# A macaron layer on one core: the shared expert's 64 rest rows in two halves of the array, with the attention order moved along

## The chip, the cores and the metric

The kernel runs on one core of a Trainium2 chip. The metric is the device time of one execution in microseconds (us), lower is better. A core has TensorE (PE, its weight loads are shown as PEld), VectorE (DVE), ScalarE (ACT), GpSimd (POOL) and SyncE (SP, which issues most DMAs). Products land in PSUM, which has eight banks here: two tiles of two banks under the tag `big`, two of one bank under `mm`, two of one bank under `aux`.

## The reference

All is float32. With 16 x 256 = 4096 tokens of 256 channels:

```python
x = x + 0.5 * ffn(layernorm(x))      # ffn adds its own input
x = x + attention(layernorm(x))
x = x + 0.5 * ffn(layernorm(x))

def ffn(inp):
    x = w_norm * inp * rsqrt(mean(inp * inp) + eps)
    # 32 experts, top 4 of each token, at most 128 tokens an expert, hidden width 176
    out = sum over chosen experts of weight * (silu(x @ w_gate[e]) * (x @ w_up[e])) @ w_down[e]
    sh = (silu(x @ sw_gate) * (x @ sw_up)) @ sw_down        # shared expert, hidden width FS = 704
    return inp + out + sigmoid(x @ w_shared_gate) * sh
```

Attention has 16 heads of width 32 (8 for keys and values), rotary positions, a tanh soft cap and a causal softmax. The change is in the shared expert, `sh`, and in the order of the attention stage.

## The kernel before

The 4096 tokens are handled as 8 groups (`NG`) of 4 tiles (`GT`) of 128 tokens. A feed-forward has a route stage (`route`, router logits and top 4), a slot stage (`slots`, which tokens each expert takes), an expert stage (`expert`, 32 times: gather by indirect DMA, gate and up products, down product, scatter-add by indirect DMA into `acc`), and the shared expert (`shared`). The attention stage has 32 units (batch element b and half of the heads m of a group), each with scores in two parts, values and, after every second unit, an output product (`project_out`).

TensorE's order is the program's order throughout; in attention that holds for DVE, ACT and POOL too, and in the expert stage for POOL.

**The shared expert.** `shared` is a generator for one group. Its hidden width 704 is five chunks of 128 and a rest of `FR` = 64. For each chunk it makes the gate and up products of 512 tokens into a `big` tile `pg` (L399), then ACT makes a tanh (L403) and DVE two operations (L404, L405), and the result stands in `act`. The rest chunk, the sixth, holds gate in 64 partitions and up in the other 64 of one half of `pg`. Then for each of the 4 tiles it adds six products (five chunks and the rest) in one PSUM tile `po` (L411, tag `mm`), and DVE adds the sum to x (L415). The rest's product runs over 128 rows, of which 64 rows of weights in `swd` are zero (L150). A float32 product is two passes, two instruction records, on TensorE.

**Filling.** `Fill` hands out the pieces of `shared` between other work. A `take(us)` adds to a budget and runs pieces until it is used up; each piece yields its assumed cost (3.4 us for a chunk, 1.7 for the rest chunk, 2.6 for a tile). The takes are listed in the constants: `ROUTE_FILL` per piece of routing, `SLOT_FILL` and `ROW_FILL` per piece of the slot stage, `FIRST_FILL`, then `EXPERT_FILL` for each of 34 steps of the expert loop. `SUM_FILL` stands behind the last expert of the first feed-forward: it covers the time in which the scatter-adds end, `read_sums` loads them, `add_sums` adds them on POOL (L474), and `moments` and `root` prepare the layer norm of attention.

**Attention's order.** `project(g)` is the chain of a group into attention: read the sums, add them, moments, the normalised rows `a` on ACT (L493), two transposes of half a group each (`pta` L503, copied by ACT to `hT` L504), then the projections `pq` (L512) and `pv` (L540). For unit k with g, j = divmod(k, 4), the loop runs pieces of group g + 1 (`mine`), group g + 2 (`ahead`) and of the routing of groups g - 1 and g - 2 (`routing`, with the transposes `pt` L267 and ACT's `xnT` L270 as one piece) at places written out by hand. `PROJECT_PIECES` says how many pieces of `mine` stand before the second part of the scores and how many behind the values.

## Time and profile before

| what | value |
|---|---|
| median of 3 runs | 1059.1 us (1058.38 to 1059.3) |
| the profiled execution | 1057.55 us |
| its span in the profile | 1055.8 us |
| granted TensorE clock | 1.0 |
| TensorE busy, idle | 1025.7 us, 30.1 us |
| `pg` products (L399) | 704 records, 318.6 us |
| `po` products (L411) | 768 records, 178.9 us |
| scatter-adds (L462) | 64, 1587 ns each on POOL |

By the trace, the route stage of the first feed-forward lies at 0 to 110 us, the slots up to 166, the experts up to 327, the way into attention up to 383, attention up to 735, and the second feed-forward behind it.

How to read it: a line of a timeline is start, duration, engine, line of the kernel, operation, tile written <- tiles read, shape, and how many instructions are merged; in brackets stands the idle time before it and what ended it. A shape like 32*128 of a matmul is rows*columns of the array in use. The duration of a matmul record runs beyond the start of the next, as the array is pipelined, so the cost of a stream is read from start to start.

### The profile page before, as it was taken

To read this page: it belongs to the slowest core of one execution; us is meant where nothing else is said; L and a number is where in the kernel's file an instruction comes from. 1 tells how busy PE (TensorE), PEld (TensorE's weight loads), DVE (VectorE), ACT (ScalarE), POOL (GpSimd) and SP (SyncE) were. 2 spreads that over 40 slices of the span, in tenths; PEclk is the share of its full clock that TensorE was granted. 3 is DMA by queue.
4 is the path that set the end of the run, shared out by engine and by line. 5 is a ranking of instruction groups with operands and counts; after the bars stand their busy time and mean duration, and the time that the engine had idled before them with its cause. 6 is when DMAs were issued, how large, how long until landed. Compare 5 with 4: busy or idle time off the path is not lost.

```text
span 1055.8 us, 15603 instructions
## 1 busy us (share of the span) xinstructions
PE 1025.7 (97%) x5432; PEld 647.2 (61%) x5432; DVE 630.9 (60%) x1684; ACT 399.1 (38%) x761; POOL 496.2 (47%) x548
## 2 busy tenths in 40 slices
PE   8999999999999999989999999999999999999998
PEld 5656656876866445545455555555566476867765
DVE  4964674544343546777878879774756635444453
ACT  3442111222221245675748476667310122232201
POOL 4410102455552478688676767564101234455450
PEclk9999999999999999999999999999999999999999
DMA  8731802878872100000101010000300157788572
GB/s 280 214 122 46 247 6 61 167 164 178 170 163 31 39 21 1 21 21 1 43 1 43 2 43 1 24 23 2 100 30 1 34 128 161 169 162 175 100 226 103
DMA packets 137869, 92.97 MB, mean 88 GB/s; under 512 B 80512, under 2 KB 135104, under 8 KB 137792
## 3 DMA queue, kind: packets, MB, share of 16 engines
q1 hardware_dynamic: 125504, 74.16, 25.6%
q0 software_dynamic: 12288, 17.83, 10.1%
q8 instruction: 43, 0.70, 0.3%
q14 instruction: 34, 0.28, 0.1%
HBM read 60.99 MB, written 30.97 MB: 87 GB/s over the span
## 4 chain that ended last, share of the span: by engine, by line
PE 87%; DVE 5%; ACT 3%; issue 1%; POOL 1%; DMA 1%; POOLq 0%; ACTq 0%
PE pg L399 26%; PE po L411 15%; PE pge L446 8%; PE pq L512 8%; PE poa L625 5%; PE sc L561 5%; PE poe L459 5%; PE y L607 3%; PE den L607 3%; PE pv L540 3%; PE pl L283 2%; PE pte L438 1%; PE pa L369 1%; ACT a L493 1%; PE pt L267 1%
## 5 line engine op out<-in xcount | busy, mean ns | idle before, releaser
L399 PE MATMUL pg<-xnT,sw 128*128 128x512 f32 x704 | 318.6, 597 | 2.0 <-DVE act L405 2.0
L399 PEld LDWEIGHTS pg<-xnT,sw 128*128 128x128 f32 x704 | 130.0, 190 | 138.3 <-issue 130.1
L462 POOL DMA_INDIRECT acc<-y,idx x64 | 101.4, 1584 | 179.6 <-DVE y L461 62.0
L411 PE MATMUL po<-swd,act 128*128 128x256 f32 x768 | 178.9, 383 | 3.9 <-DVE x L415 1.3
L403 ACT ACTIVATE act<-pg 128x512 f32<-128x512 f32 x96 | 57.2, 596 | 285.2 <-PE pg L399 285.2
L411 PEld LDWEIGHTS po<-swd,act 128*128 128x128 f32 x768 | 142.9, 190 | 34.1 <-issue 10.6
L404 DVE SCALAR_TENSOR_TENSOR act<-act,pg 128x512 f32<-128x512 f32 x96 | 65.7, 685 | 154.1 <-ACT act L403 154.1
L568 ACT ACTIVATE p<-sc 128x512 f32<-128x512 f32 (+1 forms) x128 | 97.0, 809 | 100.3 <-PE sc L561 99.8
L422 POOL DMA_INDIRECT xg<-xtab,idx x64 | 68.1, 1064 | 75.4 <-DVE idx L377 56.5
L446 PE MATMUL pge<-xgT,wgu 128*112 128x128 f32 (+1 forms) x768 | 95.9, 275 | 7.6 <-issue 5.6
L573 POOL TENSOR_SCALAR_AFFINE_SELECT p<-p 128x512 f32<-128x512 f32 x128 | 81.5, 663 | 44.2 <-ACT p L571 42.6
L571 ACT ACTIVATE p<-p 128x512 f32<-128x512 f32 (+1 forms) x128 | 101.0, 845 | 0.0
L446 PEld LDWEIGHTS pge<-xgT,wgu 128*112 128x112 f32 (+1 forms) x768 | 88.6, 182 | 11.2 <-issue 11.2
L415 DVE SCALAR_TENSOR_TENSOR x<-po,sg,x 128x256 f32<-128x256 f32 x64 | 30.9, 483 | 75.0 <-PE po L411 74.8
L441 ACT ACTIVATE xgT<-pte,wnorm 128x128 f32<-128x128 f32 x128 | 39.9, 365 | 74.8 <-PE pte L438 74.8
L405 DVE TENSOR_TENSOR act<-act,pg 128x512 f32<-128x512 f32 x96 | 65.7, 685 | 2.3
L520 POOL TENSOR_TENSOR qs<-qs,kc 128x512 f32<-128x512 f32 x48 | 61.5, 1282 | 10.3 <-DVE qs L515 10.3
L459 PE MATMUL poe<-wd,sie 112*128 112x256 f32 x256 | 65.9, 379 | 0.1
L561 PE MATMUL sc<-qT,kT 32*128 32x256 f32 (+1 forms) x512 | 64.2, 533 | 1.7 <-ACT p L568 1.3
L512 PE MATMUL pq<-hT,wq 128*128 128x512 f32 x128 | 60.9, 599 | 0.0
L625 PE MATMUL poa<-wo,yT 128*128 128x256 f32 x256 | 59.7, 386 | 1.2 <-DVE qT L519 1.2
L625 PEld LDWEIGHTS poa<-wo,yT 128*128 128x128 f32 x256 | 47.2, 190 | 18.8 <-issue 3.8
(109 smaller groups left out, 1342.6 us busy)
## 6 DMA issues: line engine op xcount, KB each, us to landing
xtab<-xr SPq DMA_DIRECT2D x16, 576.0 KB
acc<-zero SPq DMA_DIRECT2D x2, 4224.0 KB
a<-acc SPq DMA_DIRECT2D x16, 512.0 KB
wgu<-in_L_ffn_w_gate SPq DMA_DIRECT2D x64, 112.0 KB
wgu<-in_L_ffn_w_up SPq DMA_DIRECT2D x64, 112.0 KB
wd<-in_L_ffn_w_down SPq DMA_DIRECT2D x64, 112.0 KB
wgu<-in_L_ffn_w_gate SPq DMA_DIRECT2D x64, 64.0 KB
wgu<-in_L_ffn_w_up SPq DMA_DIRECT2D x64, 64.0 KB
```

The lines of the kernel that those rows point to most:

```text
L399: nc.tensor.matmul(pg[:, s, :], lhsT=sw[:, c, w0 : w0 + P], rhs=xnT[:, c, cols], start=(c == 0), stop=(c == 1))
L411: nc.tensor.matmul(po, lhsT=act[:, k, t * P : (t + 1) * P], rhs=swd[:, k, :], start=(k == 0), stop=(k == len(FC) - 1),)
L422: nc.gpsimd.indirect_dma_start(out=xg, out_offset=None, in_=xtab[n], in_offset=bass.IndirectOffsetOnAxis(ap=idx[:, e : e + 1], axis=0), bo ...
L446: nc.tensor.matmul(pg[:fw, n_, :], lhsT=wgu[:, c, w0 : w0 + fw], rhs=xgT[:, c, :], start=(c == 0), stop=(c == 1))
L459: nc.tensor.matmul(po, lhsT=si[:, k, :], rhs=wd[:, k, :], start=(k == 0), stop=(k == 1))
L462: nc.gpsimd.indirect_dma_start(out=acc[n], out_offset=bass.IndirectOffsetOnAxis(ap=idx[:, e : e + 1], axis=0), in_=y, in_offset=None, boun ...
L512: nc.tensor.matmul(pq, lhsT=weights[:, c, :], rhs=hT[:, c, :], start=(c == 0), stop=(c == 1))
L561: nc.tensor.matmul(sc[i // 2][:, i % 2, 0 : 2 * w].rearrange("p (s t) -> p s t", s=2), lhsT=kT[r, m, t0 + k0 : t0 + k0 + P], rhs=qT[r, m, ...
L568: nc.scalar.activation(parts[h], sc[h][:, :, 0 : 2 * w], AF.Tanh, scale=QK_SCALE / SOFTCAP)
L571: nc.scalar.activation(parts[h], parts[h], AF.Exp, scale=SOFTCAP)
L573: nc.gpsimd.affine_select(out=diag, in_=diag, compare_op=ALU.is_ge, fill=0.0, base=0, pattern=[[0, 4], [1, P]], channel_multiplier=-1,)
L625: nc.tensor.matmul(po, lhsT=yT[:, c // 2, c % 2, qh * P : (qh + 1) * P], rhs=wo[:, c // 2, c % 2, :], start=(c == 0), stop=(c == 3),)
```

## The change

- The rest chunk's results for tiles 0 and 1 of a group stay in partitions 0 to 63 of `act`; those for tiles 2 and 3 go to partitions 64 to 127. `swd` holds the rest's weights twice, once in each half. The rest's products of the four tiles then run one after another, 64 rows each, alternating between the halves of the array, and open the sums (`start=True`); the other five products follow.
- For that, the four tiles' sums `pos` are open at the same time: two banks of one `big` tile, and two `aux` tiles where `wide()` says so or else the two banks of a second `big` tile.
- In such a group the rest chunk is made first of the six, with its ACT and DVE work in two halves. Tiles are taken in the order 0, 2, 1, 3. Costs become 3.4 for the first tile (with all the rest products) and 2.1 for the others; `EXPERT_FILL` of the first feed-forward becomes 2.05.
- `paired` holds for groups begun in the first feed-forward and from the end of attention on; a generator is made when its group begins. Other groups keep the old way, with a memset of the empty half of `act` in place of that of `swd`.
- In attention: the pieces of `mine` are swapped in unit 1; the normalised rows of `ahead` move to the end of j = 2, the first half of its transposes to the place behind the values at j = 3, the second stays at the end; the piece of `routing` with the first transposes moves behind the fill at j = 3, but for the last units.

The diff:

```diff
--- before.py
+++ after.py
@@ -41,7 +41,7 @@
-ROUTE_FILL, SLOT_FILL, FIRST_FILL, EXPERT_FILL, SUM_FILL, PROJECT_FILL = 3.0, 1.7, 6.0, (2.15, 2.3), 17.0, 1.5
+ROUTE_FILL, SLOT_FILL, FIRST_FILL, EXPERT_FILL, SUM_FILL, PROJECT_FILL = 3.0, 1.7, 6.0, (2.05, 2.3), 17.0, 1.5
 LAST_FILL = 8.0
 MASK_FILL, ROW_FILL = 4.0, 3.2
 WARM = (9, 3)
@@ -147,8 +147,8 @@
     swd = cpool.tile([P, len(FC), C], F32, name="swd")
     nc.sync.dma_start(swd[:, 0:5, :], sw_down[0:640, :].rearrange("(c p) d -> p c d", p=P))
-    nc.gpsimd.memset(swd[FR:P, 5, :], 0.0)
-    nc.sync.dma_start(swd[0:FR, 5, :], sw_down[640:FS, :])
+    for h in range(2):
+        nc.sync.dma_start(swd[h * FR : (h + 1) * FR, 5, :], sw_down[640:FS, :])
     for g in range(2, NG):
         load_x(g)
     nc.sync.dma_start(kc[:, P:], consts[:, P:])
@@ -379,42 +379,67 @@
-    def shared(pool, g, last):
+    def shared(pool, g, last, paired, wide):
         sg = stat.tile([P, GT], F32, name="sg")
         nc.scalar.activation(sg, gate[:, g * GT : (g + 1) * GT], AF.Tanh, scale=0.5)
         nc.vector.tensor_scalar(sg, sg, 1.0, 0.125, ALU.add, ALU.mult)
         act = pool.tile([P, len(FC), GW], F32, name="act")
         cols = slice(g * GW, (g + 1) * GW)
-        for k, (f0, fw) in enumerate(FC):
+        rest = len(FC) - 1
+        for k in [rest, *range(rest)] if paired else range(rest + 1):
+            f0, fw = FC[k]
             pg = big.tile([P, 2, GW], F32, tag="big", name="pg")
-            if fw == P:
-                at = [f0, FC[-1][0] + f0]
-                b = pg[:, 1, :]
-            else:
-                at = [2 * f0]
-                b = pg[fw : 2 * fw, 0, :]
+            at = [f0, FC[-1][0] + f0] if fw == P else [2 * f0]
             for s, w0 in enumerate(at):
                 for c in range(2):
                     nc.tensor.matmul(
                         pg[:, s, :], lhsT=sw[:, c, w0 : w0 + P], rhs=xnT[:, c, cols], start=(c == 0), stop=(c == 1)
                     )
-            si = act[:fw, k, :]
-            nc.scalar.activation(act[:, k, :], pg[:, 0, :], AF.Tanh, scale=0.5)
-            nc.vector.scalar_tensor_tensor(si, si, 1.0, pg[:fw, 0, :], ALU.add, ALU.mult)
-            nc.vector.tensor_mul(si, si, b)
+            if fw == P:
+                parts = [(act[:, k, :], pg[:, 0, :], pg[:, 1, :])]
+            elif paired:
+                halves = [(slice(h * fw, (h + 1) * fw), slice(h * GW // 2, (h + 1) * GW // 2)) for h in range(2)]
+                parts = [(act[r, k, t], pg[0:fw, 0, t], pg[fw : 2 * fw, 0, t]) for r, t in halves]
+            else:
+                nc.gpsimd.memset(act[fw:P, k, :], 0.0)
+                parts = [(act[0:fw, k, :], pg[0:fw, 0, :], pg[fw : 2 * fw, 0, :])]
+            for si, a, b in parts:
+                nc.scalar.activation(si, a, AF.Tanh, scale=0.5)
+                nc.vector.scalar_tensor_tensor(si, si, 1.0, a, ALU.add, ALU.mult)
+                nc.vector.tensor_mul(si, si, b)
             yield 1.7 * len(at)
-        for t in range(GT):
+        if paired:
+            pos = big.tile([P, 2, GW], F32, tag="big", name="pos")
+            pos = [pos[:, h, 0:C] for h in range(2)]
+            if wide():
+                pos += [ps1.tile([P, C], F32, tag="aux", name="pos") for _ in range(2)]
+            else:
+                more = big.tile([P, 2, GW], F32, tag="big", name="pos")
+                pos += [more[:, h, 0:C] for h in range(2)]
+            pos = [pos[t % 2 * 2 + t // 2] for t in range(GT)]
+            for t in (0, 2, 1, 3):
+                r = slice(t // 2 * FR, (t // 2 + 1) * FR)
+                nc.tensor.matmul(
+                    pos[t], lhsT=act[r, rest, t * P : (t + 1) * P], rhs=swd[r, rest, :], start=True, stop=False
+                )
+        for n, t in enumerate((0, 2, 1, 3) if paired else range(GT)):
             i = g * GT + t
-            po = ps1.tile([P, C], F32, tag="mm", name="po")
-            for k in range(len(FC)):
+            if paired:
+                po = pos[t]
+            else:
+                po = ps1.tile([P, C], F32, tag="mm", name="po")
+            for k in range(rest if paired else rest + 1):
                 nc.tensor.matmul(
-                    po, lhsT=act[:, k, t * P : (t + 1) * P], rhs=swd[:, k, :], start=(k == 0),
-                    stop=(k == len(FC) - 1),
+                    po, lhsT=act[:, k, t * P : (t + 1) * P], rhs=swd[:, k, :], start=(k == 0 and not paired),
+                    stop=(k == (rest - 1 if paired else rest)),
                 )
             nc.vector.scalar_tensor_tensor(x[:, i, :], po, sg[:, t : t + 1], x[:, i, :], ALU.mult, ALU.add)
             last(i)
-            yield 2.6
+            yield (2.6 if not paired else 2.1 if n else 3.4)
     def expert(pool, n, e, idx, wd):
@@ -641,11 +666,15 @@
             self.done = 0
             self.left = 0.0
             self.steps = 0
-            self.works = [shared(pool, g, last) for g in range(NG)]
+            self.paired = False
+            self.wide = False
+            self.works = [None] * NG
+            self.begin = lambda g: shared(pool, g, last, self.paired, lambda: self.wide)
         def step(self):
             if self.done >= min(self.ready, NG):
                 return None
+            self.works[self.done] = self.works[self.done] or self.begin(self.done)
             cost = next(self.works[self.done], None)
             if cost is None:
                 self.done += 1
@@ -695,6 +724,7 @@
             routed.close()
             clear(0)
             load_attention()
+        fill.wide = False
         idx = pool.tile([P, E], I32, name="idx")
         fill.take(MASK_FILL)
         with tc.tile_pool(name=f"slots{n}", bufs=4, side="right", reuse_waits="tile") as sp:
@@ -722,6 +752,8 @@
     sh = ctx.enter_context(tc.tile_pool(name="shared", bufs=1))
     fill = Fill(sh)
+    fill.paired = fill.wide = True
     proj = ExitStack()
     with tc.tile_pool(name="ffn0", bufs=1) as pool:
         rows0 = ExitStack()
@@ -729,6 +761,7 @@
         first = {g: route(0, g, xrows) for g in range(NG)}
         advance(first[0], 2)
         feed_forward(0, pool, first, fill, rows0)
+        fill.paired = False
         clear(1)
         ordered = ExitStack()
         ordered.enter_context(tc.manual_schedule(engines={ET.DVE, ET.Activation, ET.Pool}))
@@ -798,7 +831,9 @@
             if k >= 2 and units[k - 2][2] == 1:
                 d = units[k - 2][:2]
                 project_out(*d, outs.pop(d))
-            advance(mine, PROJECT_PIECES[j][0])
+            before, behind = PROJECT_PIECES[j] if k != 1 else PROJECT_PIECES[j][::-1]
+            advance(mine, before)
             if k == LAST:
                 fill2.step()
             if mine is None and j % 2 == 0:
@@ -810,16 +845,15 @@
                 advance(routing.get(g - 2))
             if j == 2:
                 advance(routing.get(g - 2))
-            if j == 3:
-                advance(ahead)
             if mine is not None or j % 2:
                 unit_values()
-            if j == 3:
+            if j == 3 and k > LAST:
                 advance(routing.get(g - 1))
-            if j == 3 and k > LAST:
                 advance(routing.get(g - 2))
+            if j == 3 and k < LAST:
+                advance(ahead)
             if k == LAST - 2:
                 fill2.gates()
@@ -831,8 +865,9 @@
             elif not LAST - 5 <= k < LAST - 2:
                 spare_time(SPARE[j])
             if j == 3 and k < LAST:
+                advance(routing.get(g - 1))
                 advance(routing.get(g - 2))
-            advance(mine, PROJECT_PIECES[j][1])
+            advance(mine, behind)
             if j == 1 and g >= 1:
                 routing[g - 1] = route(1, g - 1, rows)
                 next(routing[g - 1])
@@ -840,12 +875,13 @@
                 fill2.ready = max(g - 1, 0)
             if j == 2:
                 advance(routing.get(g - 1))
+                advance(ahead)
             if j == 0:
                 advance(routing.get(g - 2))
             fill.finish(min(g + 3, NG))
             if j == 3:
-                advance(ahead, 2)
+                advance(ahead)
             elif j < 2:
                 advance(ahead)
             if j == 3 and g + 3 < NG:
@@ -854,6 +890,7 @@
         advance(routing[NG - 2], 2)
         advance(routing[NG - 1])
         fill2.ready = NG - 1
+        fill2.paired = True
         fill2.take(LAST_FILL)
         ordered.close()
     proj.close()
@@ -872,6 +909,7 @@
             for i in late:
                 if i // GT >= begun:
                     end(i, nc.gpsimd)
+            fill2.wide = True
             fill2.finish(NG)
```

## The prediction

> **What bounds the kernel now.** First the page's table of engines and its row of slices, then the chain that ended last:
>
> ```profile
> PE 1025.7 (97%) x5432; PEld 647.2 (61%) x5432; DVE 630.9 (60%) x1684; ACT 399.1 (38%) x761; POOL 496.2 (47%) x548
> PEclk9999999999999999999999999999999999999999
> PE 87%; DVE 5%; ACT 3%; issue 1%; POOL 1%; DMA 1%; POOLq 0%; ACTq 0%
> ```
>
> TensorE is the bound nearly everywhere, at full clock. A product saved there counts, unless TensorE then waits at a later point that something else sets. So I looked for such points: the waits of TensorE and the timelines around them. Three matter.
>
> ```profile
> 333.44 1.55 POOL L462 DMA_INDIRECT acc<-y,idx  x1 [2.94 <-DMA acc<-y,idx]
> 337.98 1.55 POOL L462 DMA_INDIRECT acc<-y,idx  x1 [3.00 <-DVE sg L386]
> 345.84 2.35 POOL L474 TENSOR_TENSOR x<-x,a 128x1024 f32<-128x1024 f32 x1 [6.30 <-DMA a<-acc]
> ...
> 354.27 2.06 ACT L493 ACTIVATE a<-x,hb,s 128x256 f32<-128x256 f32 x4
> 354.91 1.91 PE L503 MATMUL pta<-kc,a 128*128 128x128 f32 x8 [1.17 <-ACT a L493]
> ```
>
> In the first feed-forward the scatter-adds of GpSimd run one after the other. From scatter 3 (198.28) to scatter 31 (337.98) are 28 steps of 4.99 us; y of the last expert is ready at 327.1, 10.9 us before its scatter. Read-back, add, moments and normalisation hang on it, and TensorE waits for them at 354.91. In this stretch a faster TensorE gains nothing by itself.
>
> ```profile
> 560.35 2.06 ACT L493 ACTIVATE a<-x,hb,s 128x256 f32<-128x256 f32 x4
> 560.46 0.66 PE L267 MATMUL pt<-kc,xr 128*128 128x128 f32 x4
> 561.00 0.93 PE L503 MATMUL pta<-kc,a 128*128 128x128 f32 x4
> 562.31 0.82 ACT L270 ACTIVATE xnT<-pt,wnorm 128x256 f32<-128x256 f32 x2
> 563.19 0.66 PE L503 MATMUL pta<-kc,a 128*128 128x128 f32 x4 [1.27 <-ACT xnT L270]
> ...
> 393.06 0.70 PE L561 MATMUL sc<-qT,kT 32*128 32x256 f32 x4 [1.11 <-ACT p L568]
> ```
>
> Second and third: in attention, ScalarE's normalisation stands ahead of the copy that frees a PSUM buffer, so TensorE waits; and in unit 1 the second scores follow the first at once and wait for the tanh.
>
> ```profile
> 155.66 0.71 PE L369 MATMUL pa<-cum,sel 32*128 32x129 f32 x8
> 156.31 2.86 PE L411 MATMUL po<-swd,act 128*128 128x256 f32 x12
> 159.10 0.71 PE L369 MATMUL pa<-cum,sel 32*128 32x129 f32 x8
> 159.74 2.86 PE L411 MATMUL po<-swd,act 128*128 128x256 f32 x12
> ...
> 204.46 2.76 PE L411 MATMUL po<-swd,act 128*128 128x256 f32 x12
> 207.06 0.38 PE L438 MATMUL pte<-kc,xg 128*128 128x128 f32 x2
> ```
>
> This prices the switch to row tiles. Twelve passes (six products, two passes each) take 2.60 us from start to start in the full array (204.46 to 207.06), 0.216 a pass, but 2.79 between row-tiled groups (156.31 to 159.10). A row-tiled group of eight passes takes 0.64 or 0.65.
>
> **The rest products.** Before, each tile has a sixth product over 64 useful rows: four tiles, 8 passes, 1.73 us a group. After, tiles 0 and 2 sit in one half of the array's rows and the other, then 1 and 3. The nearest row is pa: its eight passes of 129 columns go two tiles at a time and cost four passes of 0.108, 0.43 us, plus 0.21 inside the group and 0.19 in its neighbours, 0.40 in all. So I take 4 x 0.216 + 0.40 = 1.26, a saving of 0.47 a group. The ends: no overlap at all, 1.73 + 0.40, a loss of 0.40; overlap without the 0.40, a saving of 0.87. [...]
>
> How many groups: I walked the fill budget with the costs in the code (this reproduces the order of the trace before). Groups 0 to 6 of the first feed-forward and 2 to 7 of the second begin with the flag set, 13, not 14.
>
> **The price of holding four sums.** Where the aux buffers aren't used (A2 to A6, B2 to B5; A and B are the two fills), the four sums take both big buffers. Tiles 1 and 3 then wait until the last gate chunk is consumed. That is 2.24 us after its last product (L404 starts 0.83 after, then 0.69 twice), up to 2.5 among the slot work. The rests of 0 and 2 cover 0.63. In A2 (two short slot steps between, 0.45 in the trace before) this leaves about 1.3, in A3 and B2 (one pa group, 0.74) 1.1 and 1.0, in B3 (nothing between) 1.7. In A4 to A6, B4 and B5 at least one expert's products, 2.4 us, lie between: nothing; if DVE were 1 us later there, 0.4 each. Behind the waiting product on TensorE stand tile 0's products and then the next slot's or expert's; for these wait y and the scatters (A2, A3), or only the end (B). A0, A1, B6 and B7 use aux and wait for nothing. A2, A3 and B2 are beside a tiled group, so one switch, 0.2, was there already.
>
> **Split gate, loads, memsets.** Two tanh of 64x256 for one of 128x512 (0.60), four VectorE operations near 0.42 for two of 0.69: 0.3 us more, off the path, since the rest is now made first and used last. The 64 KB of swd a second time costs one more issue on SP (0.5 to 1.2 us) ahead of six x loads, which groups 2 and later need only after 20 us: nothing, at worst 1 us. The memset of act on GpSimd (3 groups) replaces one of swd: nothing, at worst 0.5 each. In the route stage `po` no longer takes `mm` from the router: waits of 0.93, 0.32, 0.2 and 0.28 go, 1.7 us; what of it comes back as lateness of VectorE I bound by zero and all.
>
> **First feed-forward.** Groups A0 to A3 save 4 x 0.47 + 0.4, pay 2.4 for the held buffers and are rid of waits of 1.7: 1.6 us earlier at the experts (0 to 3.5). But the new budget places A4's rest gate (1.72) and chunk 3 (3.43) ahead of the first expert's y, which were behind it. Scatter 0 comes 5.15 - 1.6 = 3.55 later; scatters 1 to 3, which had waited for y (steps of 5.5, 5.8, 5.0), follow at 5.0 and catch up 1.35. The chain ends 2.2 later. At its end ScalarE is no longer held by A7's tanh (353.77), which comes over 2 us earlier: hb, ready at 353.1, is used at once, 1.1 gained. TensorE's transposes start at 356.0 for 354.9, but A7's rest gate (1.72) now lies before them, in the wait. Net -0.6 us (-2.5 to +1.5). The savings of A4 to A6 are swallowed by that wait.
>
> **Attention.** Unit 1: two projection pieces (3.4) between the scores remove 1.11 + 0.21. The normalisation moves to the end of j = 2, where ScalarE was idle 2.19 us before the tanh at 553.51; one half of the transposes goes behind the values. In unit 3 the eight transposes, 2.3 us with their wait from 420.8 to 423.1, need 1.0: 1.3 gained. In the three j = 3 units without fill (waits 0.84, 1.27, 1.27) only a 0.58 copy stands ahead: 0.3 left of each, 2.4 gained. Sum 5.0; I take 4.5 (bounds 7 and -2). Behind the moved normalisation on ScalarE's queue is the tanh of unit 3; if it came 2 us late, poa (3.65) covers 1.6. On DVE, POOL and SP the moved steps issue what they did.
>
> **Second feed-forward.** TensorE sets the end here: scatters end at 1008 and the output adds follow products until 1052. 6 x 0.47 + 0.2 + 0.3 (waits at 843 and the tail) - 2.7 held = -0.6 (-3 to +2).
>
> **Sum.** -0.6 - 4.5 - 0.6 = -5.7. The profiled execution took 1057.55 (span 1055.8): 1051.85. The median of the runs is 1.55 higher, so against it 1059.1 - 5.7 = 1053.4.
>
> **Rivals.** (1) Attention's waits only move: VectorE is 70 to 80% busy there and several pieces change neighbours. Then -1.2, 1057.9. For it: three of the stalls follow work of VectorE or GpSimd; against: the waits shown name ScalarE. (2) The held buffers cost double, since VectorE takes up the chunk later: 2.4 more through the chain and 2.7 in the second feed-forward, 1058.5. For it: the trace has consumption 3.66 us after the chunk in the route stage. (3) Slower: the two 64-row halves do not overlap. Each group then costs 0.87 more; in the ten groups whose time counts (A0 to A3 through the chain, B2 to B7) 8.7, so +3.0: 1062.1. The sign turns once 0.57 of the 0.87 is lost. No row has 64-row tiles, but pa and sc overlap fully, so I give it and unnamed losses of its size little. (4) The count is 14: 0.5 us less, inside the forecast; the walk of the budget speaks against it.
>
> **How the numbers follow.** A difference of 0.2%, 2.1 us, is about what a measurement of this kernel can tell from none. The forecast has 0.58 (its own range 1050 to 1057), of which 0.56 faster and 0.02 within 0.2%; rivals 1 and 2 have 0.12 and 0.10, together 0.10 faster, 0.11 within, 0.01 slower; rival 3, with unnamed losses of its size, 0.20, of which 0.02 within. Faster 0.66, same 0.15, slower 0.19. The range, 1048.5 to 1061, takes in rivals 1 and 2 and leaves out a fast end (attention's gains in full and an early chain, under 0.08) and the worst part of rival 3 (0.12).
>
> **What would show it.** In the profile after: 104 matmul records of 64*128 (112 if 14 groups), eight in about 0.97 us and the passes behind them 0.19 longer; no wait of pta on xnT above 0.5 us and none of the second scores near 391; a wait of 3 us or so before the first pta near 355; waits of the rest products on L405 of 0.6 to 1.7 us in four groups; scatter 0 near 185.5 and scatter 31 near 340. I am wrong if 64*128 passes follow each other at 0.216 with no overlap, if new waits stand in units 2 to 24 of attention, or if the first pta starts after 358.

## The result: slower by 0.33%, and the profile after

The changed kernel takes 1061.93 us (median of 19 runs, 1058.88 to 1065.68) against 1058.4 us for the kernel before on the same chip (19 runs). The ratio is 1.0033, 95% interval 1.0023 to 1.0043. The forecast was 1053.4, in a range of 1048.5 to 1061. The profiled execution took 1061.56 us with a span of 1059.8, which is 4.0 us more than before.

The page after: the table of engines, the slices of the granted clock, and the chain that ended last.

```profile
PE 1019.6 (96%) x5432; PEld 636.2 (60%) x5432; DVE 638.2 (60%) x1710; ACT 402.9 (38%) x774; POOL 495.9 (47%) x550
PEclk9999999999999999999999999999999999999999
PE 83%; DVE 7%; DMA 4%; issue 2%; ACT 1%; POOL 1%; POOLq 0%; ACTq 0%; DVEq 0%
```

TensorE is busy 6.1 us less and still the span grew. In the chain it fell from 87% to 83%, while VectorE rose to 7% and DMA to 4%: TensorE now waits for others. The clock row still shows only nines: the two short stretches at half clock that are shown below do not show in slices of 26 us. The view of waits (us in total, times, longest) says for whom it waits:

```profile
PE pg L399 <- DVE act L413: 6.3, 3, 5.4
PE pos L426 <- DVE act L413: 4.9, 4, 1.5
...
PE pos L436 <- DVE x L440: 3.4, 7, 0.6
PE pa L369 <- DVE row L375: 2.6, 1, 2.6
```

The same rows before:

```profile
PE pg L399 <- DVE act L405: 2.0, 3, 0.9
PE po L411 <- DVE x L415: 1.3, 4, 0.4
```

The rest products and `pa` had no such row there. L413 is VectorE's last step of a gate chunk, L426 the rest product of 64 rows, L436 the other down products, L440 the addition to x. A table of points of the program, in us from the start of the span, shows where the time went. The columns are the shift against the kernel before; e1, e9, e10 and e13 are explained below.

| point | before | after | e1 | e9 | e10 | e13 |
|---|---|---|---|---|---|---|
| slot stage begins (first `pc`) | 110.14 | +3.59 | -0.53 | -0.77 | -0.40 | +0.64 |
| first gather | 155.31 | +8.11 | -0.55 | -0.46 | -0.41 | +0.63 |
| scatter 0 | 181.93 | +12.15 | -0.54 | +1.61 | -0.41 | +0.63 |
| scatter 31 | 337.98 | +11.88 | +0.90 | -0.30 | -1.40 | +0.35 |
| first `pta` | 354.91 | +11.05 | -0.53 | +2.06 | -0.41 | +0.63 |
| first scores | 383.55 | +8.78 | -0.52 | +3.15 | -0.74 | +0.30 |
| last scores | 735.56 | +2.50 | -6.81 | -3.00 | -6.91 | -5.92 |
| last product | 1051.85 | +3.55 | -6.80 | -1.95 | -6.41 | -6.82 |

The first feed-forward lost 11 us. Then 2.3 us come back on the way to the first scores, attention gives 6.3, and the second feed-forward costs 1.05. The columns compare single executions, and between scatter 0 and scatter 31 the same 31 steps take 153.4 to 157.5 us in the 16 profiles, so a difference of 2 us there is not put down to an edit.

**The start.** The timeline of the changed kernel, from the first chunks of group 0:

```profile
12.48 5.40 PE L399 MATMUL pg<-xnT,sw 128*128 128x512 f32 x12
...
17.70 0.40 DVE L412 SCALAR_TENSOR_TENSOR act<-act,pg 64x256 f32<-64x256 f32 x1
...
20.10 0.29 DVE L299 TENSOR_REDUCE tot<-ex 128x4 f32<-128x128 f32 x1 [1.53 <-ACT ex L294]
20.58 1.00 ACT L411 ACTIVATE act<-pg 64x256 f32<-64x256 f32 x2
21.94 0.42 DVE L412 SCALAR_TENSOR_TENSOR act<-act,pg 64x256 f32<-64x256 f32 x1
23.17 1.14 DVE L413 TENSOR_TENSOR act<-act,pg 64x256 f32<-64x256 f32 x2
23.74 6.31 PE L399 MATMUL pg<-xnT,sw 128*128 128x512 f32 x8 [5.42 <-DVE act L413]
```

The rest chunk's buffer is free only when both halves have gone through ScalarE and VectorE. The second tanh comes six us after the first, since router work stands between them and VectorE is itself held 1.53 us by the softmax (L299). So the next chunk but one waits 5.42 us. And then eight products, 3.60 us at full clock, take 6.31. The view of windows (window, length, busy time and count of PE, PEld, DVE, ACT and POOL, granted clock, DMA) has the reason:

```profile
18.00:23.70 5.70, 0.32 (x3) 0.08 (x1) 4.01 (x15) 3.97 (x9) 1.11 (x4) 0.87 1.10 361
23.70:30.00 6.30, 6.26 (x10) 2.66 (x10) 4.78 (x27) 2.07 (x4) 2.49 (x6) 0.58 0.55 173
```

The clock granted after the wait is 0.58 on the mean. The same two windows of the kernel before:

```profile
18.00:23.70 5.70, 4.75 (x15) 2.19 (x14) 3.58 (x15) 3.47 (x8) 2.26 (x5) 1.00 1.09 360
23.70:30.00 6.30, 5.57 (x26) 3.55 (x25) 5.16 (x28) 3.76 (x8) 1.33 (x5) 1.00 0.74 208
```

TensorE is busy 4.75 and 5.57 us there, and the clock is at 1.00.

**The slots.** Between these two steps of the slot stage the fill gives out no piece of the shared expert:

```profile
140.77 0.71 PE L369 MATMUL pa<-cum,sel 32*128 32x129 f32 x8
144.11 1.39 PE L369 MATMUL pa<-cum,sel 32*128 32x129 f32 x8 [2.63 <-DVE row L375]
145.44 4.79 PE L399 MATMUL pg<-xnT,sw 128*128 128x512 f32 x7
```

The second `pa` waits 2.63 us for VectorE. Its eight passes then take 1.33 us from start to start instead of 0.65, still at full clock: the first two do not run as a pair, and the third waits 0.13 us more for VectorE's next operation on `row`. The half clock lies behind them, from 145.11 to 148.52 us by the trace's clock records (0.66 on the mean in 144 to 149): seven gate products take 4.79 us, where seven take 3.27 at full clock (e6, at 117.10 us).

**What was forecast and came.** The rest product itself. The grouped view by form, and the start of the tail, where nothing is held:

```profile
L426 PE MATMUL pos<-swd,act 64*128 64x256 f32 x104 | 15.8, 410 | 4.9 <-DVE act L413 4.9
```

```profile
1014.61 1.13 PE L426 MATMUL pos<-swd,act 64*128 64x256 f32 x8
1015.67 2.43 PE L436 MATMUL pos<-swd,act 128*128 128x256 f32 x10
```

There are 104 records, so 13 groups. Eight passes take 1.06 us from start to start, and their neighbours 0.09 before and 0.10 behind: 1.25 in all, where the forecast had 1.26. And attention; here is the unit that the prediction showed:

```profile
555.96 2.07 ACT L518 ACTIVATE a<-x,hb,s 128x256 f32<-128x256 f32 x4
...
565.20 0.66 PE L528 MATMUL pta<-kc,a 128*128 128x128 f32 x4
565.69 0.49 PE L267 MATMUL pt<-kc,xr 128*128 128x128 f32 x3
```

The normalisation lies 9 us ahead of the transposes instead of less than one. Of the wait of 1.27 us 0.24 is left, at the second half of `pta` (566.53), for the copy to `hT`.

### The profile page after: what moved, and what is told of

Same layout as the page of the kernel before. It is cut to its first block, busy times and chain, and to the rows that moved or that the text cites. A ratio compares the mean times of both kernels' runs of the same rounds, so it can differ in the third digit from the quotient of the medians.

```text
span 1059.8 us, 15615 instructions
## 1 busy us (share of the span) xinstructions
PE 1019.6 (96%) x5432; PEld 636.2 (60%) x5432; DVE 638.2 (60%) x1710; ACT 402.9 (38%) x774; POOL 495.9 (47%) x550
## 4 chain that ended last, share of the span: by engine, by line
PE 83%; DVE 7%; DMA 4%; issue 2%; ACT 1%; POOL 1%; POOLq 0%; ACTq 0%; DVEq 0%
PE pg L399 26%; PE pos L436 9%; PE pq L537 7%; PE pge L471 7%; PE poa L650 5%; PE sc L586 5%; PE poe L484 4%; PE y L632 3%; PE po L436 3%; PE den L632 3%; PE pv L565 3%; DMA acc<-y,idx 2%; PE pl L283 2%; PE pte L463 1%; DMA xg<-xtab,idx 1%
## 5 line engine op out<-in xcount | busy, mean ns | idle before, releaser
L399 PE MATMUL pg<-xnT,sw 128*128 128x512 f32 x704 | 322.5, 603 | 6.3 <-DVE act L413 6.3
L411 ACT ACTIVATE act<-pg 128x512 f32<-128x512 f32 (+2 forms) x109 | 59.3, 544 | 295.7 <-PE pg L399 269.9
L412 DVE SCALAR_TENSOR_TENSOR act<-act,pg 128x512 f32<-128x512 f32 (+2 forms) x109 | 67.6, 620 | 156.2 <-ACT act L411 127.7
L436 PE MATMUL pos<-swd,act 128*128 128x256 f32 x520 | 122.5, 384 | 4.1 <-DVE x L440 3.4
L436 PEld LDWEIGHTS pos<-swd,act 128*128 128x128 f32 x520 | 96.2, 190 | 23.4 <-DVE x L440 5.8
L413 DVE TENSOR_TENSOR act<-act,pg 128x512 f32<-128x512 f32 (+2 forms) x109 | 67.8, 622 | 2.9
L440 DVE SCALAR_TENSOR_TENSOR x<-pos,sg,x 128x256 f32<-128x256 f32 x52 | 25.1, 483 | 64.8 <-PE pos L436 59.0
L477 DVE SCALAR_TENSOR_TENSOR sie<-sie,pge 112x256 f32<-112x256 f32 x64 | 26.9, 420 | 53.1 <-ACT sie L476 41.4
```

What stands on the lines that cost most here:

```text
L399: nc.tensor.matmul(pg[:, s, :], lhsT=sw[:, c, w0 : w0 + P], rhs=xnT[:, c, cols], start=(c == 0), stop=(c == 1))
L436: nc.tensor.matmul(po, lhsT=act[:, k, t * P : (t + 1) * P], rhs=swd[:, k, :], start=(k == 0 and not paired), stop=(k == (rest - 1 if paire ...
```

## The experiments

Letters as in the prediction: A0 to A7 are the groups of the first fill, B0 to B7 those of the second. The 95% intervals reach 0.1 to 0.3% to each side; where a difference is smaller, the trace's points are given. The runs were timed on several chips; beside them the kernel before took 1058.0 to 1058.8 us, so two edits' medians compare to about 1 us. All edits are to the changed kernel unless said otherwise.

**e1_order: attention's new order alone, in the kernel before.** The edit is the hunks of the attention loop.

> The kernel before with the new order of attention alone (unit 1 swapped, normalised rows and transposes moved). Theory: the order is worth what the trace of the changed kernel shows between the first scores and the last ones, 6.3 us (8.78 late at unit 0, 2.50 late at the last unit), so about 6 us faster than before, 1052 to 1053, with the waits of pta on xnT and of the second scores in unit 1 gone. Rival: those 6.3 us are only lateness given back, because in the changed kernel the sums were late and attention had slack; then the order alone brings 2 us or less, 1056 to 1058.

Measured: 1051.43 us, ratio 0.9929 [0.9908, 0.9949]. The shift is -0.52 at the first scores and -6.81 at the last; it stays to the end. All of the gain belongs to this part. The rest of the change costs 10.5 us.

**e2_first_old: group A0 in its old form.** The budget is raised so that the rest lies as in the changed kernel.

> The changed kernel, but the first group of the first feed-forward keeps the old form (rest chunk last, one sum a tile); the budget is moved by 0.65 ahead of the slots, so that every piece from there on lies where it lay. Theory: the stall of 5.4 us near 18 us and the half clock behind it (granted 0.58 from 23.7 to 30) come from the rest chunk in front, whose release of its PSUM buffer passes ScalarE and VectorE twice; without it the router's second group comes 6 us or more earlier, and the experts' first result and the first transposes of attention 3 to 5 us earlier: 1057.5 to 1059. Rival: VectorE is the limit of the first 50 us in any order, and the stall comes back elsewhere there: less than 1 us, 1061 to 1062.

```diff
-lambda g: shared(pool, g, last, self.paired, ...)
+lambda g: shared(pool, g, last, self.paired and g > 0, ...)
+        if n == 0:
+            fill.left += 0.65
         fill.take(MASK_FILL)
```

Measured: 1058.36 us, ratio 0.9992 [0.998, 1.0003], 3.6 us better than the change. The timeline still has a wait:

```profile
20.76 0.29 DVE L299 TENSOR_REDUCE tot<-ex 128x4 f32<-128x128 f32 x1 [2.29 <-ACT ex L294]
```

VectorE still has the reduction L299 ahead of the next group's moments, as after and not as before, and TensorE waits 2.02 us at 23.92. The router of group 1 starts 4.6 us earlier than in the change (29.15 for 33.76), but at the start of the slots 1.5 of the 3.6 us are back (+2.08), and 1.5 more come between scatter 0 and 31. So the form of A0 is most of the loss at its own place and under half of it at the slots, and something else moved VectorE's order.

**e3_warm: twelve products of zeros in the gap at the start.** They are to keep the clock up and do no useful work.

> The changed kernel with twelve products of zeros (24 passes, 5.2 us) on TensorE ahead of the second chunk of the first group, where TensorE stands idle 5.4 us. Nothing is computed with them. Theory: the idle time is what halves the clock, so with them the granted clock stays 1.0 there and the eight passes behind take 3.4 instead of 6.3 us: the router's second group comes 2.5 to 3.5 us earlier, and the end about 2 to 3 us. Rival: the clock is lowered by something else (the start, DMA), then the passes stay near 0.85 us and the end does not move.

```diff
             f0, fw = FC[k]
+            if paired and g == 0 and k == 1:
+                warm(12)
```

Measured: 1063.81 us, ratio 1.0043 [1.0028, 1.0058]. In the gap the theory is right: the clock is 1.00 in both windows (18 to 30 us), and the router of group 1 comes 2.7 us earlier than in the change (31.09 for 33.76). But TensorE then waits 2.48 and 1.54 us at 48 and 51, the clock falls there (0.74 on the mean in 48 to 54), and the slot stage begins at +7.01. The forecast of the end failed.

**e4_cover: one us less budget ahead of the slots**, so that a piece falls behind the step that had none.

> The changed kernel with the fill budget 1.0 us lower ahead of the slot stage of the first feed-forward: a piece then lies behind each of the four slot steps 3.0 to 3.3, as in the kernel before, where the changed one has none behind step 3.0. Theory: the wait of pa on row (2.6 us at 141.5 us) and the half clock behind it (granted 0.66 from 144 to 149) go, so the first expert result comes 4 us or more earlier and the end 3 to 4 us: 1058 to 1059. Rival: the wait is VectorE's own lateness among the slot work and moves to the next step: less than 1 us.

```diff
+        if n == 0:
+            fill.left += -1.0
         fill.take(MASK_FILL)
```

Measured: 1060.29 us, ratio 1.0013 [0.9999, 1.0026].

```profile
144.00:149.00 5.00, 5.00 (x19) 2.26 (x18) 3.74 (x10) 0.60 (x1) 0.00 (x0) 1.00 0.00 0
355.00:365.00 10.00, 7.99 (x22) 3.31 (x22) 4.97 (x13) 4.21 (x8) 1.68 (x4) 0.94 0.02 5
```

The hole in the slots and its half clock are gone (1.00 for 0.66), and scatter 0 comes 6.1 us earlier than in the change. At the first `pta` 4.7 of it are left. Between there and the first scores this execution loses 1.3 against before, where the change gained 2.3: its clock there falls (0.94). The median gains 1.6.

**e5_swd_late: the second load of the rest's weights behind the loads of x.**

> The changed kernel with the second load of the rest's swd rows behind the loads of x instead of ahead of them. Theory: the order of VectorE and ScalarE is planned automatically in this stage, from estimated arrivals; the extra load ahead of x moves the moments of the third group behind the sum of the router's exponentials, and VectorE then waits for ScalarE. With the load behind, the stall near 18 us shrinks by 2 us or more, the half clock gets shorter, and the experts' first result comes 2 to 4 us earlier: 1058.5 to 1060. Rival: only the rest chunk in front makes the stall, and it stays near 5 us: 1061 to 1062.

```diff
     for g in range(2, NG):
         load_x(g)
+    nc.sync.dma_start(swd[FR : 2 * FR, 5, :], sw_down[640:FS, :])
     nc.sync.dma_start(kc[:, P:], consts[:, P:])
```

Measured: 1059.66 us, ratio 1.0002 [0.999, 1.0014]: 2.3 us better than the change. VectorE has L299 behind the moments again, as before, the longest wait at the start falls from 5.4 to 4.2 us, and the slot stage begins 2.2 us earlier than in the change (+1.35). A 64 KB load that TensorE needs much later cost this by its place ahead of six loads of x. That the order of VectorE was planned from its arrival is argued; the run shows that the order goes back with the load.

**e6_first_fixed: e2, e5 and e4 together.**

> The changed kernel with three things put right in the first feed-forward: its first group in the old form, the second swd load behind the loads of x, and the fill budget 1.0 us lower ahead of the slots, so that each of the steps 3.0 to 3.3 has a piece behind it. Theory: start and slots together cost the first feed-forward 8 to 9 us; the first expert result then comes within 3 us of the kernel before, attention keeps its 6 to 7 us, and the time is 1052 to 1055. Rival: rest products in six groups cost the first feed-forward by themselves (held buffers, switches); then the first expert result is still 6 us or more late, 1056 to 1058.

Measured: 1060.28 us, ratio 1.0014 [1.0005, 1.0023]; not the gain that was expected.

```profile
111.21 0.29 PE L332 MATMUL pc<-triu,mask 128*32 128x128 bf16 x8 [2.97 <-DVE mask L316]
```

With 1.0 us less the hole went to another step, that of the masks; the first three gate products behind it take 2.44 us, where eight ahead of it take 3.68 us (104.56), and the mean clock of the run is 0.993. A shift of the budget that suits one place opens another.

**e7_second: first feed-forward old, rest products only in B2 to B7.** With the second load late as in e5, `EXPERT_FILL` at 2.15, and the new attention order.

> The new order of attention, and rest products side by side in groups 2 to 7 of the second feed-forward alone; the first feed-forward is as before (EXPERT_FILL 2.15), with the second swd load behind the loads of x. Against the kernel with the order alone (1051.4): by the blind forecast -0.6 us; by the trace of the changed kernel, which loses 1.1 us from the last attention unit to the end, +1. So 1050.8 or 1052.5. A rival in which the rest products bring their 0.47 us a group without the held buffers' cost would give 1048.6.

```diff
-    fill.paired = fill.wide = True
```

Measured: 1061.42 us, ratio 1.0022 [1.0012, 1.0032]. This did not isolate the second feed-forward. Groups in the old form clear half of `act` on GpSimd (L408), and in the expert stage GpSimd keeps the program's order. The timeline of GpSimd, and of TensorE:

```profile
264.32 1.59 POOL L487 DMA_INDIRECT acc<-y,idx  x1 [1.70 <-DMA acc<-y,idx]
265.39 1.06 POOL L408 MEMSET act<- 64x512 f32 x1
```

```profile
266.50 0.70 PE L436 MATMUL po<-swd,act 128*128 128x256 f32 x2 [1.91 <-POOL act L408]
267.26 2.46 PE L471 MATMUL pge<-xgT,wgu 128*112 128x128 f32 x12
```

The memset stands behind a scatter that waits for its predecessor, and the down product waits for the memset; behind it twelve gate products take 2.46 us, in the kernel before 1.48 (207.27), and the mean clock of the run is 0.996. The wait is there twice.

**e8_second_apart: e7, but two sums at a time**, tiles 0 and 2 first, then 1 and 3, each pair in one big buffer.

> As the one with rest products in the second feed-forward alone, but where the sums take big buffers (groups 2 to 5) the rest products of tiles 1 and 3 come after tiles 0 and 2, so that only one big buffer is needed at a time; the pieces' assumed costs are left as they are. Theory: the waits of the held buffers (1.4 to 1.9 us in groups 2 and 3) go, against one more switch of 0.4 us in each of four groups: 1 to 1.5 us faster than with all four sums open. Rival: the wait only moves to tile 0, whose last product needs the same chunk: no difference, or 1.6 us slower by the switches.

```diff
+            open_sums((0, 2, 1, 3) if at_once else (0, 2))
 ...
+                if n == 2 and not at_once:
+                    more = big.tile([P, 2, GW], F32, tag="big", name="pos")
+                    pos += [more[:, h, 0:C] for h in range(2)]
+                    open_sums((1, 3))
```

Measured: 1059.89 us, ratio 1.0003 [0.9994, 1.0013], with the same memset in its first half. In the second feed-forward alone it is 1.5 us better than e7. That needed a cleaner run, e13.

**e9_first_fixed2: A0 old, the load late, 0.3 us less budget, and zeros made by ScalarE** (a tanh whose scale is 0 in partitions 64 to 127) in place of the memset.

> A second try at a first feed-forward without the holes: first group in the old form, second swd load behind the loads of x, and the fill budget only 0.3 us lower ahead of the slots. By the walk of the budget a piece then lies behind the mask step (the first try had moved the hole there: 3.56 us idle ahead of pc and half the clock behind it) and behind each of the slot steps 3.0 to 3.3. Groups in the old form get the zeros of their empty half from the tanh itself (scale 0 there) instead of a memset on GpSimd. Theory: with the holes gone the first expert result is at most 4 us later than before, and the time is 1053 to 1056. Rival: the held buffers alone (1.5 us in groups 2 and 3, with halved clock behind) and the changed start keep it 6 us or more late: 1057 to 1060.

```diff
-                nc.gpsimd.memset(act[fw:P, k, :], 0.0)
+                nc.scalar.activation(act[:, k, :], pg[:, 0, :], AF.Tanh, scale=half)
```

Measured: 1055.85 us, ratio 0.9975 [0.9966, 0.9985]: 6.1 us better than the change. Ahead of the experts all holes are gone (-0.46 at the first gather), and scatter 0 is at +1.61. One stretch at lower clock is left, behind the first `pta` (0.91 on the mean in 355 to 360, 0.75 in 360 to 365):

```profile
356.97 1.91 PE L532 MATMUL pta<-kc,a 128*128 128x128 f32 x8 [1.18 <-ACT a L522]
359.56 3.41 PE L541 MATMUL pq<-hT,wk 128*128 128x512 f32 x4 [0.68 <-ACT hT L533]
```

Four products take 3.25 us to the next start, in e1 1.82. So 9 of the 11 us lost in the first feed-forward can be kept. A gain does not appear there; TensorE waits for `a`, so what it saved ahead of this wait does not count.

**e10_second_clean: e7 with these zeros.**

> As the one with rest products in groups 2 to 7 of the second feed-forward alone, but the zeros of the old form come from the tanh (scale 0 in the empty half) and not from a memset on GpSimd, which in that run waited behind the scatter-adds and held TensorE for 2.3 and 1.2 us. Theory: the first feed-forward is then as in the kernel with the order alone, and the difference to it (1051.4) is that of the second feed-forward: +1 us, 1052 to 1053. Rival: rest products cost more than 3 us there, or the first feed-forward is disturbed by the second load of swd by itself: 1055 or more.

Measured: 1051.32 us, ratio 0.9939 [0.9918, 0.996], as e1. From the last scores to the end it takes 0.5 us more than e1. Six groups of rest products bring nothing. The timeline of B3:

```profile
834.49 0.70 PE L430 MATMUL pos<-swd,act 64*128 64x256 f32 x4
836.69 0.70 PE L430 MATMUL pos<-swd,act 64*128 64x256 f32 x4 [1.50 <-DVE act L417]
837.32 2.43 PE L440 MATMUL pos<-swd,act 128*128 128x256 f32 x10
...
840.33 2.42 PE L440 MATMUL pos<-swd,act 128*128 128x256 f32 x10 [0.36 <-DVE x L444]
```

The held buffer costs 1.50 here and 1.12 in B2 (2.6 in all), and in four groups the second tile waits for the addition of the first (2.1 us). All waits of TensorE behind the last scores sum to 9.3 us here and to 5.4 in e1. That is 3.9 more, against a saving of 2.8 (six groups at 0.47): a balance of +1.1 for a measured +0.5. The part on the second feed-forward below finds the rest.

**e11_late_four: rest products only in B4 to B7**, and the first feed-forward old.

> The order of attention, and rest products side by side only in groups 4 to 7 of the second feed-forward, where an expert's products or the aux buffers leave no wait for a held buffer; old form elsewhere, zeros from the tanh. Theory: 4 x 0.47 us less than the order alone: 1049.5. Rival: the pieces in new places cost as much as the products save: 1051 to 1052.

Measured: 1052.32 us, ratio 0.9934 [0.9917, 0.9951]. The theory's 1.9 us are not seen: from the last scores to the end it takes 0.6 more than e1. The sum of waits there is 7.8 us, 2.4 more than in e1; 1.7 of it are waits of `pos` for x, the term that the theory did not have. Less the saving of 1.9 that gives +0.5. The time as a whole says little, since the profile has half clocks in the first half of the program (0.97 on the mean up to 50 us, 0.93 in 350 to 400).

**e12_first_experts: rest products only in A4 to A6.**

> The order of attention, and rest products side by side only in groups 4 to 6 of the first feed-forward, which run beside its experts; old form elsewhere, zeros from the tanh. Theory of the blind forecast: the chain of scatter-adds sets the end of that stage, so the 1.4 us of TensorE are swallowed by its wait ahead of the first transposes of attention: 1051 to 1052, as with the order alone, with that wait longer by 1 to 2 us. Rival: they count: 1050.

Measured: 1054.55 us, ratio 0.9959 [0.9944, 0.9974], 3.1 us worse than e1. The first `pta` comes 1.9 us later than in e1, and the wait before it grows from 1.18 to 1.77 us, so the saving does not count, as the theory had it. But the scatters are not what ends last: scatter 31 comes 1.7 us earlier than in e1 (337.19 for 338.88), and the moments that follow the sums stand 2.4 us later on VectorE, behind the two operations of a gate chunk (start at 351.31 for 348.86). A4's rest chunk ahead of the first y makes scatter 0 1.2 us later than before, and behind the longer wait comes a half clock:

```profile
352.00:358.00 6.00, 4.07 (x14) 1.56 (x12) 2.68 (x8) 3.02 (x6) 1.68 (x4) 1.00 0.00 0
358.00:363.00 5.00, 3.92 (x8) 1.75 (x7) 1.41 (x4) 1.18 (x3) 0.00 (x0) 0.66 0.30 105
```

e1 has 1.00 in both windows, with TensorE busy 3.99 and 5.00 us.

**e13_second_apart_clean: e10 with e8's edit.**

> The kernel of e10_second_clean (new attention order, rest products only in groups B2 to B7, zeros made by a tanh of scale 0 in the other groups), but where the aux buffers are not used (B2 to B5) a group opens only two sums first, those of tiles 0 and 2 in one big buffer, and the sums of tiles 1 and 3 after these two are finished. Theory (the held buffers eat the saving): in e10 the second feed-forward, from the last scores of attention to the end, lost 0.5 us against e1_order, with waits of 1.5 and 1.9 us before the third rest product in B2 and B3. Both waits go, and two more switches of tile mode in each of four groups come, 4 x 0.4 = 1.6 us at most; e8_second_apart was 1.5 us better than e7_second from that edit. So the second feed-forward ends 1.0 to 1.9 us earlier than in e10, and the time is 1050.0 against e1_order's 1051.4 and e10's 1051.3. Rival (the waits only hide other lateness: the output adds and the scatters end as before, or the extra switches cost what the waits did): the second feed-forward ends within 0.4 us of e10's and the time is 1051.3 or more.

Measured: 1050.06 us (1048.48 to 1054.75, 6 runs), ratio 0.9914 [0.9886, 0.9942]. The timeline of B3 again:

```profile
834.55 0.70 PE L429 MATMUL pos<-swd,act 64*128 64x256 f32 x4
835.19 2.42 PE L446 MATMUL pos<-swd,act 128*128 128x256 f32 x10
```

The wait of 1.50 is gone, that of B2 too. From the last scores to the end it takes 315.39 us, for 316.79 in e10 and 316.30 in e1: 1.4 better than e10, as the theory said, and 0.9 better than the old form. So the held buffers ate most of the saving. The sum of waits fell by 2.4 us (6.8 for 9.3) and 1.4 came back. Counted from start to start without waits, a group's products in B4 and B5 take 10.11 us for 9.81 in e10: the second switch of tile mode costs 0.30 there. In B2 and B3, which the held buffer had cut in two already, it costs nothing (+0.03 and -0.07). This profile has a half clock at the start (0.97 up to 50 us), hence its +0.6 in the first column of points.

**e14_turn_about: e13 with B6 and B7 in the order 0, 1, 2, 3.**

> The kernel of e13_second_apart_clean, with the tiles of B6 and B7 (where four sums are open in one big and two aux buffers) finished in the order 0, 1, 2, 3 instead of 0, 2, 1, 3: two sums that follow each other then never lie in the same big tile. Theory: in the traces of the change, e10 and e13, the second tile of a group waits 0.58 us for VectorE's addition of the first (pos behind x, twice in B6 and B7), because both sums lie in halves of one big tile and a wait is for the whole tile. Both waits go, the second feed-forward from the last scores of attention to the end takes 1.2 us less than e13's 315.4 us, so 314.2, and the time is 1049 against 1050.1. Rival: TensorE waits there for something else that VectorE's addition only happens to end (the weights, the sum's own products), and then the waits of 0.58 stay in some place of the group and the second feed-forward takes 315.4 us within 0.4.

```diff
-        for n, t in enumerate((0, 2, 1, 3) if paired else range(GT)):
+        for n, t in enumerate((0, 2, 1, 3) if paired and not at_once else range(GT)):
```

Measured: 1052.28 us (1049.12 to 1055.35, 7 runs), ratio 0.9951 [0.993, 0.9972]. e13's timeline of B6 first, then that of this run:

```profile
1005.94 2.43 PE L446 MATMUL pos<-swd,act 128*128 128x256 f32 x10
1008.95 6.74 PE L446 MATMUL pos<-swd,act 128*128 128x256 f32 x30 [0.58 <-DVE x L450]
```

```profile
1003.75 8.90 PE L446 MATMUL pos<-swd,act 128*128 128x256 f32 x40
1019.57 13.97 PE L402 MATMUL pg<-xnT,sw 128*128 128x512 f32 x32 [1.78 <-DVE act L417]
```

Both waits of 0.58 are gone: 40 passes follow each other. Two sums in one buffer were the reason. But the gate chunk behind now waits 1.78 us, since VectorE has output additions (L807 there) ahead of the rest chunk's. The stretch to the end takes 315.62 us for 315.39, so the gain became another wait. The lowest runs, 1049.1, are as e13's lowest; the medians of e13 and e14 are not told apart by their intervals.

Of all versions e1, e10 and e13 have the lowest medians, 7 to 9 us below the kernel before and 10 to 12 below the change; their intervals overlap, and those of e11 and e14 overlap them. So no whole time shows a gain from rest products beside e1. By the trace e8 and e13, with two sums at a time, have the shortest second feed-forwards (315.16 and 315.39 us).

## Why the prediction was wrong

**Attention: right in mechanism, and too small.** Forecast -4.5, measured -6.3 in the change and in e1 alone. By e1's trace the waits of TensorE between the first and last scores fell by 4.2 us (7.4 to 3.2); from start to start the transposes `pta` take 1.7 less and the scores 0.8. These last terms were in part missing from the sum. Rival 1, that the waits only move, falls.

**Rest products: right.** 13 groups, and 1.25 us a group for 1.26. Rival 3, no overlap of the two halves, falls: its 8 passes would take 1.73. What failed is not the saving of 0.47 but what was set against it.

**First feed-forward: forecast -0.6 by the first scores, measured +8.8.** Four steps of it failed.

1. "Split gate ... off the path, since the rest is now made first and used last." Its results are used last, but its buffer is needed by the next chunk but one. Where VectorE and ScalarE run router work between, that cost 5.42 us of waiting in A0. e2 gives 3.6 us of the median back, of which its trace shows 1.5 ahead of the slots.
2. "Nothing, at worst 1 us" for the second load of `swd`. e5 shows 2.3 in the median and 2.2 at the start of the slots: with the load ahead of x VectorE's order at the start is another.
3. The walk of the fill budget was used for counts of groups and for what lies ahead of y. It also says which slot steps have no piece behind them, and that was not priced: 2.63 us at 141.5, and from the start of the slots to the first gather 4.5 in all, with A2's and A3's held buffers (2.3) and the half clock in it. e4 takes the hole away: the same stretch loses 0.3, and scatter 0 is 6.1 us earlier.
4. The sum had no clock in it. Each of the two holes was followed by half clock, for 6.8 and 3.4 us. That added 2.7 us to the first (eight products, 6.31 for 3.60) and 1.5 to the second (seven, 4.79 for 3.27), and in e12 it made a saving that lengthened a wait a loss.

The forecast of what lay ahead of y (5.15) measured 4.0, but the scatters caught up 0.3 instead of 1.35, since steps of 5.1, 4.6 and 6.2 us follow scatter 0 where 5.0 each were forecast. Scatter 0 came at 194.08 (forecast 185.5), scatter 31 at 349.86 (340), the first `pta` at 365.96 (after 358 was the prediction's own sign of being wrong). Behind it 2.3 us came back; 1.7 were forecast for A7's rest chunk, and no run places the other 0.6. That the savings of A4 to A6 do not count agrees with e12, though there VectorE's moments end last and not the scatters. That the scatters set this stretch is thus not shown. A wait of about 3 us was forecast for the first `pta`; in the change TensorE does not wait there, and 44 gate products run up to it. A tanh of such a chunk stood last in front of `a` on ScalarE (`a` starts at 364.94, `hb` is ready at 364.21), as in the kernel before (354.27 and 353.10): the 1.1 us that were to be gained by its leaving became 0.4. Three waits of `pte` for a gather, 3.6 us in all between 292 and 328, were not followed up.

**Held buffers: right in size.** Forecast 1.3, 1.1, 1.0 and 1.7 in A2, A3, B2 and B3. The waits before the third rest product measured 1.18, 1.12, 1.12 and 1.50. Rival 2, twice that, falls.

**Second feed-forward: forecast -0.6, measured +1.05** (+0.5 in e10, without the first half's troubles). The term that was missing is the wait of a tile for VectorE's addition of the one before, when both lie in one big buffer: 0.36 to 0.58 us in four groups, 2.1 us in all. e14 shows the cause for B6 and B7. The sum of waits behind the last scores is 9.8 us in the change, 4.4 more than in e1; less the saving of 2.8 this would give +1.6. The saving is larger than 2.8. From start to start, waits left out, the shared expert's down products (L411 before, L426 and L436 in the change) take 3.6 us less than in e1, and all else 0.3 more: +1.05. In e10 they are +3.93 of waits, -3.46 and no more than +0.02: +0.49. The largest piece is B5, 10.66 to 9.81 us, where in the old form the products of the first tile alone take 2.89 us for 2.60.

**Slower had 0.19 of the chance** and hung on the rest products. The loss came from where the prediction said "nothing".

## What to carry to other kernels

When a change reorders the pieces that fill TensorE's pauses, go through every pause of the stage and ask which piece now covers it, rather than only whether TensorE's work adds up; an uncovered pause costs itself and, in several runs here, a half clock behind it (stretches of 6.8 and 3.4 us in the changed kernel). Price a buffer by the time until its last reader is done, with that reader's whole queue in front of it, and count sums that are open together as one buffer if they share a tile. Test the parts of a change apart: here one part gave all of the gain (7 us), and the other cost 10; with its buffers, its zeros and its place changed it cost nothing that the times can tell.

## What the runs showed of the hardware

- **Half clock after some waits.** The clock records of the changed kernel's profile show half clock from 22.23 us for 6.827 us and from 145.11 us for 3.413 us; a pass of a gate product takes 0.853 us from start to start there (24.73 to 25.58) and 0.43 at full clock (1013.65 to 1014.08). The first stretch begins 3.9 us into the wait of 5.42 us, the second 1.0 us after the end of the wait of 2.63 us. Shorter waits were followed by it in some runs and not in others. e9 and e1 have the same two waits at the first `pta` and behind it, 1.18 and 0.68 us: in e9 the clock behind them is 0.91 and 0.75 on the mean (355 to 360 and 360 to 365), in e1 it stays at 1.00 (352 to 363). TensorE's busy time ahead does not tell such cases apart either: in 352 to 358 it is 4.07 us in e12, where a clock of 0.66 follows (358 to 363), and 3.99 us in e1. What decides is not shown here.
- **Single runs differ by their clock.** Each run has its mean clock on record. Of 41 runs of the kernel before beside e1, 20 with 0.999 or 1.000 took 1057.1 to 1058.8 us, 16 with 0.998 took 1058.9 on the mean, and five with 0.993 took 1062.5 to 1063.8. A stretch of 3.413 us at half clock lowers the mean by 0.0016 (an estimate from that length in a span of 1056). All 19 runs of the changed kernel have 0.992 to 0.995, by this estimate 11 to 17 us at half clock each; the profiled one has 0.995. So the half clock belongs to the kernel and not to the one execution that was profiled.
- **The switch to 64-row tiles costs as that to 32-row tiles.** The neighbours of eight passes grew by 0.09 and 0.10 us, 0.19 as by `pa` before. The passes of the two halves overlap in pairs: at 1014.6 us the two of a pair start 7 ns apart, and the eight take 1.06 us, where four full passes of 0.216 take 0.86.
- **An order that is planned automatically can turn with an edit elsewhere.** In the route stage, one load of 64 KB at another place put a reduction ahead of the moments on VectorE, and products of zeros (e3) were followed by waits of 2.48 and 1.54 us at a place 25 us later.
